# Turning the scans through DRAM: 256-byte writes into 16 KB rows, whole rows read back

## The chip, the cores and the metric

One core of a Trainium2 chip runs the whole program in one launch. The metric is the device time of that launch in microseconds. A run is repeated; one further execution is recorded by the hardware profiler. Engines are called as in the profile: PE (matmul), DVE (vector), ACT (scalar), POOL (GpSimd) and SP, which here only issues DMA transfers. SP and ACT each have one hardware DMA queue; both use the core's 16 DMA engines.

## The reference

An image `x` of shape (4, 48, 256, 256) in fp32 passes four residual layers, each `x = x + f(groupnorm(x))`. Layer 0 is a channel attention with depthwise convolutions, layer 1 a gated pointwise network, and layers 2 and 3, which the change concerns, are scans. A scan layer normalises its input and then runs four recurrences. Each step adds a 5-tap convolution of the line before (48 channels to 48) to the present line:

```python
def step(w, b):
    def f(carry, inp):
        nxt = inp + _conv1d(carry, w, b)
        return (nxt, nxt)
    return f
_, d_rest = jax.lax.scan(step(down_w, down_b), d0, xs[1:])     # rows, top to bottom
_, u_rest = jax.lax.scan(step(down_w, down_b), u0, seq)        # rows, bottom to top
_, r_rest = jax.lax.scan(step(right_w, right_b), r0, ws[1:])   # columns, left to right
_, l_rest = jax.lax.scan(step(left_w, left_b), l0, R[Ww - 2::-1])  # columns, right to left
```

The first two go over 256 rows, the last two over 256 columns of what the first two left. At the end the layer's own input is added (the residual).

## The kernel before

The program is one list of calls; a scheduler of the framework orders the instructions of each engine and adds the waits, except where `pin` keeps the written order. Layers 0 and 1 fill the first 2885 us and are interleaved. Then `scans` (from L1023) does reference layers 2 and 3 as `layer` 0 and 1 of one loop (L1143).

**One step.** A line (a row or a column) is held as 3 x 128 partitions: 8 positions along the line times 48 channels make 384, cut into three parts `m`; the free dimension is 128 long (32 positions within a piece times 4 images). `step` (L1084) is nine 128x128 fp32 matmuls into three PSUM banks and three DVE operations (L1103) that add bias and present line. The next step needs this step's result, so the steps form one chain over PE and DVE.

**Blocks.** 32 lines are a block, numbered J for rows and n for columns (`NBK` = 8). A block is 384 x 4096 values, 6.29 MB; 256 B, 64 values, is the part of one channel and row that lies in one piece of a column position. Buffers in SBUF: two big tiles of 3 x 4096 per partition (`c_big`), three slots of 4096 and three ring tiles of eight lines (`RING`). A ring tile of eight lines is filled (rows: normalised by ACT, L1172; L1170 shares the first one over ACT, DVE and POOL), stepped through in place, and spilled to DRAM in packets of 12 KB (rows `Dd`, L1241; columns `Rd`, L1353); the way back loads it again (L1298 on SP, L1452 on ACT). The last five stay (`KEEP`).

**From rows to columns and back**, all through DRAM, by plain DMAs with rearranged access patterns:

- Layer 2's input comes in row blocks from `x2r` (`load_x2`, L1122). Its residual is copied into column order by POOL (`copy_rows`, L1190: 12 copies of 1024 values a block into slots) and written to `Y0` in 24 DMAs a block (L1196), 256 B each, in steps of 2 KB.
- In the up scan ACT keeps each row in a big tile `u` (`keep_row`, L1253); a full block goes to `U` in packets of 2 KB (`write_U`, L1258; ten DMAs, `pieces_of_lines`). Column block n is read from `U` in packets of 256 B (`load_C`, L1266 for one block of rows, L1271 for several). POOL picks the columns out of it (`fetch`, L1314). For the last row block, the part that column block 0 needs is written and read first (L1301, L1302).
- In the left scan POOL adds the finished columns to the residual, the stage tile `s` (`add_line`, L1382). `stage_of` (L1360) loads it: in layer 2 from `Y0` in packets of 2 KB (L1372), in layer 3 from `Y1` in rows of 16 KB (L1369). In layer 2 the sum is the next layer's input: `write_Y` (L1384) writes it to `Y1` by column blocks in 16 KB rows, DVE takes its statistics (L1439), and `load_y` (L1128) reads row blocks of it in packets of 256 B, the first one in two parts (L1404 and L1457). `Y1` has rows of 4096 + 64 values, 48 of them for each of 64 groups, so that step from group to group is 48 x 4160 x 4 = 798,720 B. `U` and `Y0` have rows of exactly 16 KB and steps of 786,432 B from row to row of a block.
- In layer 3 the sum is the output (L1428).

**SP's queue.** Nearly all of these are issued by SP, in one order. A transfer that must wait for a buffer or for data holds up all that stand behind it. The instructions' waits show eight semaphores for these transfers in rotation, so that a transfer also waits for the one eight before it.

**The gated layer** (reference layer 1, `gated_layer` from L662) works on 32 items, each a band of 32 rows of one image. In a `tick`, SP loads `tok` (L751) and `xr` (L863), POOL sorts the result into `yr` (L897), and two DMAs write it to `x2r` (L909). Normally that write is put off to the beginning of the next tick; once the layer 0 work that it is interleaved with has ended (`alone`), the write is issued at once (L915).

Of the kernel before, what the change touches and what calls it, by code (L numbers as in the profile page):

```python
# [26 lines left out]
NPOS = 8  # L27
# [634 lines left out]
def gated_layer(ctx, tc, banks, p_small, x1, x2r, w1, w2, dw, ends, pw, cols, b2, k, coef1, coef2):  # L662
# [206 lines left out]
    def output(c, ip, alone):  # L869
# [45 lines left out]
        if alone:  # L915
            unwritten.pop()()
# [106 lines left out]
def scans(ctx, tc, x2r, out, wts, biases, dram, k, coef2, spare):  # L1023
# [104 lines left out]
    def load_y(t, J, n0=0, n1=NBK, queues=(nc.sync,)):  # L1128
        v = t.rearrange("p (m q e) -> p m q e", m=3, e=64)
        src = Y1.rearrange("q c e -> c q e")  # L1130
        for q, (j, c0, c1, m, p0, np_) in enumerate(pieces):
            at = 512 * j + 64 * J
            queues[q % len(queues)].dma_start(  # L1133
                v[p0 : p0 + np_, m, 8 * n0 : 8 * n1], src[c0:c1, 8 * n0 : 8 * n1, at : at + 64]
            )

    load_x2(xin, 0)
    Y0 = dram.tile([NPOS, 3 * 128, NBK, NBK, 64], F32, tag="Y0", name="Y0")
    Y1 = dram.tile([NBK * NPOS, C, SLOT + 64], F32, tag="Y1", name="Y1")
    both = (nc.sync, nc.scalar)  # L1140
    coefs = spread(coef2[:C].rearrange("p b s -> p (b s)"), "spread0")

    for layer in range(2):  # L1143
# [3 lines left out]
        U = dram.tile([NPOS, 3 * 128, NBK, NBK * 64], F32, tag=f"U{layer}", name="U")  # L1147
# [32 lines left out]
        def copy_rows(x, J):  # L1180

            def pieces_of(m):
                got = {}

                def one(b):
                    if b == 0:
                        got["t"] = slot_of.take("xr")
                    src = x.rearrange("p (m b i a g) -> p m b i g a", m=3, b=B, a=4, g=4)[:, m, b]
                    dst = got["t"][0].rearrange("p (i b g a) -> p b i g a", b=B, g=4, a=4)[:, b]
                    pin(nc.gpsimd.tensor_copy(dst, src))  # L1190

                def write():
                    t, h = got["t"]
                    v = t.rearrange("p (i n e) -> p i n e", i=NPOS, n=NBK)
                    for i in range(NPOS):
                        nc.sync.dma_start(Y0[i, chunk(m), :, J, :], v[:, slot_of_row(i)])  # L1196
                    give(h)

                return [lambda b=b: one(b) for b in range(B)] + [write]
# [10 lines left out]
        for a in range(32):  # L1210
            t, h = D[a]
            J, al = a // 4, a % 4
            if al == 0:
# [3 lines left out]
                if J + 1 < NBK:  # L1217
# [3 lines left out]
                    else:  # L1221
                        load_y(xnext[0], J + 1)
# [4 lines left out]
            if layer == 0 and al == 0:  # L1227
                copy_rows(xin, J)
            if a == 24:
                load_weights(ways.index((layer, 1)))  # L1230
            for i in range(NPOS):
# [6 lines left out]
                if copies and i % 2 == 0:  # L1238
                    copies.pop(0)()
# [11 lines left out]
        def keep_row(t, i, al, line):  # L1251
            v = t.rearrange("p (m i n a) -> p m i n a", m=3, i=NPOS, a=4)
            nc.scalar.copy(v[:, :, i, :, al], line)  # L1253

        def write_U(t, J, lo, hi):
# [385 lines left out]
```

## Time and profile before

| | us |
|---|---|
| median of 3 runs | 7228.17 |
| lowest, highest | 7224.77, 7231.26 |
| profiled execution, its own time | 7225.91 |
| its span in the profile | 7223.8 |
| PE busy in the span | 6764.5 |
| layers 0 and 1, about | 0 to 2885 |
| layer 2: down and up, right and left | 2900.0 to 3926.4, 3944.5 to 5018.9 |
| layer 3: down and up, right and left | 5063.5 to 6167.5, 6186.3 to 7215.4 |

In the profile a stretch of time is given as start:end in microseconds from the span's start. Busy times of an engine are summed over instructions; beside them stands their number. The DMA share is the mean busy share of the 16 DMA engines, and since packets on one engine overlap it can pass 1. A name such as `x<-Y` is what a transfer writes and reads, with buffer numbers left out: `Y` stands for `Y0` and `Y1`. "SPq" is the SP engine's DMA queue: the time in a row of it is how long SP was held issuing, not how long the data took. fp32 matmuls run in two passes, so nine of a step are 18 records.

### The profile page before, as it was taken

How to read it: one execution, taken by the hardware profiler on the slowest of the kernel's cores; microseconds unless marked ns; L12 is line 12 of the kernel's file. 1: busy time of each engine (PE TensorE's matmuls, PEld its weight loads, DVE VectorE, ACT ScalarE, POOL GpSimd, SP SyncE). 2: the span in 40 equal slices, each digit the busy share in tenths (PEclk: the TensorE clock that was granted, in tenths of full speed). 3: DMA queues.
4: the chain of work that ended last, by engine and by line, in shares of the span. 5: the costliest groups of instructions: out<-in, count | busy, mean ns of one | idle time of the engine just before them, and what ended most of it. 6: DMA issues, size and time to landing. Idle time of an engine off the chain costs nothing.

```text
span 7223.8 us, 125645 instructions
## 1 busy us (share of the span) xinstructions
PE 6764.5 (94%) x51694; PEld 5407.3 (75%) x51694; DVE 3764.6 (52%) x8893; ACT 1751.0 (24%) x1994; POOL 2143.7 (30%) x4268
## 2 busy tenths in 40 slices
PE   4999999999999965999999999996888999999999
PEld 3666653333333322999999999996888999899999
DVE  7887643355555555444444445664444444444444
ACT  0111112243434443444443000000535343100000
POOL 0101000033333344432000555764000000455677
PEclk9999999999999987999999999998999999999999
DMA  7651124566666675897567868898998267776675
GB/s 174 161 156 62 70 71 144 169 173 178 188 180 182 173 170 148 264 294 201 168 196 193 216 190 162 247 240 216 190 169 169 88 202 210 193 197 187 257 286 208
DMA packets 1177535, 1325.47 MB, mean 183 GB/s; under 512 B 831809, under 2 KB 1006401, under 8 KB 1125121
## 3 DMA queue, kind: packets, MB, share of 16 engines
q1 hardware_dynamic: 1163424, 1229.27, 63.0%
q10 hardware_dynamic: 13440, 87.84, 3.6%
q8 instruction: 406, 6.65, 0.4%
q14 instruction: 169, 1.38, 0.1%
q0 software_dynamic: 96, 0.33, 0.0%
HBM read 793.72 MB, written 522.19 MB: 182 GB/s over the span
## 4 chain that ended last, share of the span: by engine, by line
PE 55%; DMA 3%; SPq 3%; DVE 2%; POOL 1%; issue 1%; ACT 1%; ACTq 0%; POOLq 0%; DVEq 0%
PE ps L1097 54%; SPq L1133 2%; DMA D<-d 1%; ACT d L1172 1%; POOL s L1382 1%; DMA tok<-x 0%; DVE y L892 0%; DVE v L810 0%; POOL yr L897 0%; DMA near<-n 0%; DVE st L925 0%; PE ph L711 0%; DMA r<-R 0%; DMA x2r<-yr 0%; PE ptok L764 0%
## 5 line engine op out<-in xcount | busy, mean ns | idle before, releaser
L1097 PE MATMUL ps<-d,w 128*128 128x128 f32 (+1 forms) x18360 | 2070.3, 276 | 101.4 <-DVE d L1103 62.4
L1097 PEld LDWEIGHTS ps<-d,w 128*128 128x128 f32 x18360 | 2065.4, 193 | 106.2 <-DVE d L1103 66.1
L1097 PE MATMUL ps<-r,w 128*128 128x128 f32 (+1 forms) x18360 | 2071.7, 276 | 68.4 <-POOL r L1314 35.4
L1097 PEld LDWEIGHTS ps<-r,w 128*128 128x128 f32 x18360 | 2065.9, 193 | 74.3 <-DVE r L1103 37.9
L1103 DVE SCALAR_TENSOR_TENSOR d<-ps,b,d 128x128 f32<-128x128 f32 x3054 | 979.7, 349 | 1153.2 <-PE ps L1097 1074.8
L1382 POOL TENSOR_TENSOR s<-s,r 128x128 f32<-128x128 f32 x1536 | 745.4, 520 | 334.9 <-DVE r L1103 332.9
L1103 DVE SCALAR_TENSOR_TENSOR r<-ps,b,pre 128x128 f32<-128x128 f32 x1530 | 490.1, 348 | 581.3 <-PE ps L1097 581.1
L1103 DVE SCALAR_TENSOR_TENSOR r<-ps,b,r 128x128 f32<-128x128 f32 x1530 | 490.2, 348 | 459.6 <-PE ps L1097 432.5
L588 PE MATMUL py<-x1n,wy 128*96 128x512 f32 x1536 | 700.9, 606 | 2.4 <-POOL x2n L544 0.5
L1314 POOL COPY pre<-c 128x128 f32<-128x128 f32 x1530 | 558.4, 403 | 468.8 <-DVE r L1103 466.2
L1172 ACT ACTIVATE d<-x,spread 128x256 f32<-128x256 f32 x752 | 510.7, 826 | 543.3 <-DMA D<-d 325.7
L289 PE MATMUL acc<-moving,raw 128*48 128x240 f32 x4096 | 598.6, 367 | 11.6 <-DVE moving L275 9.9
L289 PE MATMUL acc<-moving,still 128*48 128x240 f32 x4096 | 588.8, 367 | 0.2
L1253 ACT COPY u<-d 128x384 f32<-128x384 f32 x510 | 448.8, 899 | 573.4 <-DVE d L1103 510.9
L588 PEld LDWEIGHTS py<-x1n,wy 128*96 128x96 f32 x1536 | 245.3, 165 | 418.6 <-issue 376.3
L1314 POOL COPY r<-c 128x128 f32<-128x128 f32 x6 | 2.4, 395 | 1689.2 <-DMA c<-U 1689.2
L611 DVE TENSOR_TENSOR y<-py,t 96x512 f32<-96x512 f32 x256 | 173.3, 677 | 565.5 <-PE py L597 565.5
L289 PEld LDWEIGHTS acc<-moving,raw 128*48 128x48 f32 x4096 | 317.6, 123 | 147.4 <-DVE moving L275 10.0
L289 PEld LDWEIGHTS acc<-moving,still 128*48 128x48 f32 x4096 | 320.3, 123 | 137.1 <-ACT acc_sb L306 1.5
L897 POOL COPY yr<-y 96x256 f32<-96x256 f32 x512 | 315.9, 661 | 202.0 <-DVE y L892 192.0
L597 PE MATMUL py<-x2n,wy 64*96 64x512 f32 x1536 | 361.9, 601 | 0.0
L597 PEld LDWEIGHTS py<-x2n,wy 64*96 64x96 f32 x1536 | 116.7, 158 | 234.4 <-issue 230.3
(194 smaller groups left out, 4244.9 us busy)
## 6 DMA issues: line engine op xcount, KB each, us to landing
t<-in_xc SPq DMA_DIRECT2D x64, 1536.0 KB
c<-U SPq DMA_DIRECT2D x348, 256.0 KB
D<-d SPq DMA_DIRECT2D x54, 1536.0 KB
d<-D SPq DMA_DIRECT2D x54, 1536.0 KB
R<-r SPq DMA_DIRECT2D x54, 1536.0 KB
r<-R ACTq DMA_DIRECT2D x54, 1536.0 KB
U<-u SPq DMA_DIRECT2D x84, 768.0 KB
sx<-in_x SPq DMA_DIRECT2D x128, 384.0 KB
```

What stands on the lines that cost most here:

```text
L289: nc.tensor.matmul(acc[i][64 * s : 64 * s + C], lhsT=still[i][:, w * C : (w + 1) * C], rhs=moving[:, i, w * C : (w + 5) * C], start=u == 0 ...
L588: nc.tensor.matmul(ps, lhsT=held["w"][0][:, dx], rhs=x1n[:, 2 * c : 2 * c + 2, dx : dx + W], start=dx == 0, stop=False)
L597: nc.tensor.matmul(held["ps"][q + 2 * s], lhsT=held["w"][1][here, dx], rhs=x2n[here, 2 * q : 2 * q + 2, dx : dx + W], start=False, stop=dx ...
L611: nc.vector.tensor_add(part, held["ps"][c], t1[:P, 2 * c : 2 * c + 2, :])
L897: nc.gpsimd.tensor_copy(yrs[c][:, :, 2 * i2 + ip, :].rearrange("p j (n a g) -> p j n a g", a=4, g=4)[:, :, :, al], y[:, i2, al].rearrange( ...
L1097: nc.tensor.matmul(ps[m][:, here], lhsT=w[:, n, :], rhs=old[:, q, there], start=first, stop=last)
L1103: nc.vector.scalar_tensor_tensor(new[:, m], ps[m], bias[:, m : m + 1], inp[:, m], ALU.add, ALU.add)
L1133: queues[q % len(queues)].dma_start(v[p0 : p0 + np_, m, 8 * n0 : 8 * n1], src[c0:c1, 8 * n0 : 8 * n1, at : at + 64])
L1172: pin(nc.scalar.activation(dst, src, AF.Identity, bias=g[:, 1:2], scale=g[:, 0:1]))
L1253: nc.scalar.copy(v[:, :, i, :, al], line)
L1314: nc.gpsimd.tensor_copy(dst[:, m].rearrange("p (J a b) -> p J a b", J=NBK, b=B), v[:, m, j, :, gl].rearrange("p J b a -> p J a b"),)
L1382: nc.gpsimd.tensor_add(v, v, line[:, m].rearrange("p (J a b) -> p J a b", J=NBK, b=B))
```

## The change

- `U`, `Y0` and `Y1` get one layout, that of `Y1`: 64 groups of 48 rows of 4096 + 64 values. There is a `U` and a `Y0` for each layer.
- All writes to them go through `scatter`: ten DMAs a block, each of up to 48 partitions times 64 packets of 256 B, in steps of 798,720 B from packet to packet. This takes in the writes to `U` and `Y1`, 2 KB and 16 KB packets before.
- All reads go through `gather`: three DMAs of 128 rows of 16 KB. Where less than a block is read (for the last row blocks of `U` and the first block of `Y1`), parts of these rows are.
- Layer 3's residual no longer comes from `Y1`: its input blocks, once in SBUF, are scattered to a second `Y0` as soon as a block begins.
- `copy_rows` makes 48 copies of 256 values a block, two a step, in the new order; its three writes are three, four and three scatter pieces.
- `keep_row` writes its row into another order of the same tile.
- At the turn to columns, only the first of the ten pieces is written ahead of the first column's read; the rest of the first column block is written and read next, on both queues.
- In the gated layer, only the last item's write is issued at once.

```diff
-        if alone:
+        if c + 1 == len(items):
             unwritten.pop()()
...
-    def load_y(t, J, n0=0, n1=NBK, queues=(nc.sync,)):
-        v = t.rearrange("p (m q e) -> p m q e", m=3, e=64)
-        src = Y1.rearrange("q c e -> c q e")
-        for q, (j, c0, c1, m, p0, np_) in enumerate(pieces):
-            at = 512 * j + 64 * J
-            queues[q % len(queues)].dma_start(
-                v[p0 : p0 + np_, m, 8 * n0 : 8 * n1], src[c0:c1, 8 * n0 : 8 * n1, at : at + 64]
+    ROW = SLOT + 64
+    scratch = lambda name: dram.tile([NBK * NPOS, C, ROW], F32, tag=name, name=name)
+    both = (nc.sync, nc.scalar)
+    thirds = lambda t: [t[:, m * SLOT : (m + 1) * SLOT] for m in range(3)]
+
+    def scatter(dst, at, ts, lo=0, hi=64, queues=(nc.sync,), some=pieces):
+
+        for n, (pos, c0, c1, m, p0, np_) in enumerate(some):
+            queues[n % len(queues)].dma_start(
+                dst.rearrange("q c e -> c q e")[c0:c1, lo:hi, at(pos) : at(pos) + 64],
+                ts[m].rearrange("p (q e) -> p q e", e=64)[p0 : p0 + np_, lo:hi],
             )
 
+    def gather(ts, src, block, lo=0, hi=SLOT, inner=None, queues=(nc.sync,)):
+
+        rows = src.rearrange("(n i) c e -> n (i c) e", i=NPOS)[block]
+        for m in range(3):
+            to, of = ts[m][:, lo:hi], rows[chunk(m), lo:hi]
+            if inner:
+                to, of = (x.rearrange("p (j e) -> p j e", e=512)[:, :, inner[0] : inner[1]] for x in (to, of))
+            queues[m % len(queues)].dma_start(to, of)
...
-                    v = t.rearrange("p (i n e) -> p i n e", i=NPOS, n=NBK)
-                    for i in range(NPOS):
-                        nc.sync.dma_start(Y0[i, chunk(m), :, J, :], v[:, slot_of_row(i)])
+                    scatter(Y0, lambda j: 512 * J + 64 * j, {m: t}, some=[p for p in pieces if p[3] == m])
                     give(h)
 
-                return [lambda b=b: one(b) for b in range(B)] + [write]
+                return [lambda b=b, al=al: one(b, al) for b in range(B) for al in range(4)] + [write]
...
-                        load_y(xnext[0], J + 1)
+                        gather(thirds(xnext[0]), Y1, J + 1)
...
-            if layer == 0 and al == 0:
-                copy_rows(xin, J)
+            if al == 0:
+                if layer == 0:
+                    copy_rows(xin, J)
+                else:
+                    scatter(Y0, lambda j: 512 * j + 64 * J, thirds(xin))
...
+            v = t.rearrange("p (m n i e a) -> p m n i e a", m=3, n=NBK, i=NPOS, a=4)
+            nc.scalar.copy(v[:, :, :, i, :, al], line.rearrange("p m (n e) -> p m n e", n=NBK))
+
+        def write_U(t, J, **how):
+            scatter(U, lambda j: 512 * j + 64 * J, thirds(t), **how)
...
                 if row == 40:
                     near = big_tile("c")
-                    load_C(near[0], 0, 2, NBK)
+                    gather(thirds(near[0]), U, 0, inner=(128, 512))
                 if row == 32:
-                    load_C(near[0], 0, 1, 2)
+                    gather(thirds(near[0]), U, 0, inner=(64, 128))
...
-        write_U(ut, 0, 0, 64)
-        load_C(near[0], 0, 0, 1)
-        write_U(ut, 0, 64, 512)
+        write_U(ut, 0, hi=8, some=pieces[:1])
+        gather(thirds(near[0]), U, 0, hi=512, inner=(0, 64), queues=both)
+        write_U(ut, 0, hi=8, some=pieces[1:], queues=both)
+        gather(thirds(near[0]), U, 0, lo=512, inner=(0, 64), queues=both)
+        write_U(ut, 0, lo=8)
...
-                load_C(near[0], n + 1, 0, NBK)
+                gather(thirds(near[0]), U, n + 1)
...
-            if layer == 1:
-                for m in range(3):
-                    nc.sync.dma_start(s[m], Y1.rearrange("(n i) c e -> n (i c) e", n=NBK)[n, chunk(m), :SLOT])
-                return s, hs
-            for i, c0, c1, m, p0, np_ in pieces:
-                nc.sync.dma_start(
-                    s[m].rearrange("p (j e) -> p j e", j=NPOS)[p0 : p0 + np_],
-                    Y0[i].rearrange("(j c) n J e -> c j n (J e)", c=C)[c0:c1, :, n, :],
-                )
+            gather(s, Y0, n)
             return s, hs
...
+        def write_Y(s, n, **how):
+            scatter(Y1, lambda i: 512 * n + 64 * i, s, **how)
...
-                load_y(xnext[0], 0, 1, NBK)
+                gather(thirds(xnext[0]), Y1, 0, lo=512)
...
-            write_Y(s, 0, 0, 64, both)
-            load_y(xnext[0], 0, 0, 1, both)
-            write_Y(s, 0, 64, 512)
+            write_Y(s, 0, hi=8, queues=both)
+            gather(thirds(xnext[0]), Y1, 0, hi=512, queues=both)
+            write_Y(s, 0, lo=8)
```

## The prediction

> **What bounds the kernel now.** I read the page first, then PE's busy time stage by stage, then who ended PE's waits in the bad stages, then the SP queue there, and last the DMA engines in windows that hold one kind of transfer. The page says that PE is the bound and that the DMA traffic is mostly tiny:
>
> ```profile
> PE 6764.5 (94%) x51694; PEld 5407.3 (75%) x51694; DVE 3764.6 (52%) x8893; ACT 1751.0 (24%) x1994; POOL 2143.7 (30%) x4268
> DMA packets 1177535, 1325.47 MB, mean 183 GB/s; under 512 B 831809, under 2 KB 1006401, under 8 KB 1125121
> ```
>
> The busy table by stretches (start:end, length, PE busy (matmuls), ..., clock, DMA share, GB/s):
>
> ```profile
> 2900.00:3926.40 1026.40, 1026.32 (x9172) 1025.83 (x9172) 490.24 (x1530) 448.52 (x616) 188.86 (x96) 1.00 0.72 217
> 3926.40:3944.50 18.10, 0.80 (x2) 0.50 (x2) 0.30 (x1) 0.87 (x1) 1.77 (x6) 0.61 0.93 210
> 3944.50:4820.00 875.50, 875.49 (x7801) 873.54 (x7802) 489.74 (x1422) 0.00 (x0) 529.70 (x1281) 1.00 0.82 213
> 4820.00:5018.90 198.90, 164.73 (x1380) 163.59 (x1378) 108.96 (x291) 0.00 (x0) 120.01 (x249) 0.91 0.77 217
> 5018.90:5063.50 44.60, 4.43 (x24) 3.96 (x24) 15.13 (x34) 3.25 (x6) 2.73 (x3) 0.54 1.16 190
> 5063.50:5580.00 516.50, 454.00 (x3922) 450.34 (x3923) 209.81 (x653) 242.01 (x333) 1.69 (x3) 0.92 1.06 181
> 6167.50:6186.30 18.80, 0.80 (x3) 0.51 (x3) 0.35 (x1) 0.86 (x1) 1.81 (x6) 0.55 0.95 213
> ```
>
> First row: 510 scan steps in 1026.4 us, PE never idle, so 2.01 us a step and 64.4 us for a block of 32 rows. All that a change of transfers can win in the scans is PE's idle time: 17 us at each of the two turns from rows to columns, 34 in the end of layer 2's left scan, 40 between the layers, 62.5 in layer 3's down scan, 171 in all. Who ends it in layer 3's down scan, and the SP queue in one block of it (start, length, line, transfers):
>
> ```profile
> PE ps L1097 <- DVE d L1103: 62.4, 14, 17.2
> ...
> 5297.49 0.32 SPq L1241 DMA_DIRECT2D D<-d  x1
> 5297.87 30.67 SPq L1133 DMA_DIRECT2D x<-Y  x9
> 5328.65 17.43 SPq L1241 DMA_DIRECT2D D<-d  x3
> ```
>
> DVE is blamed, but the chain of work runs SP L1133, D<-d, ACT L1172: spills of finished rows stand in SP's queue behind 256-byte reads of Y1, a ring tile is not freed, and ACT fills the next rows late. The rates, mean or in 40 bins, in the order: Y0's 256 B writes in 2 KB steps (2908); U's 2 KB writes (3483); Y0's 2 KB reads (4405, idle after half); the 256 B reads of Y1 (5092); U's 256 B writes at the turn (6171.5); whole rows of 16 KB (6700):
>
> ```profile
> GB/s 0 0 0 0 0 145 290 288 296 284 288 285 287 293 287 293 282 285 293 287 293 287 282 291 291 288 291 284 284 295 285 295 287 278 295 288 291 288 282 289
> ...
> DMA packets 2135, 4.16 MB, mean 260 GB/s; under 512 B 113, under 2 KB 113, under 8 KB 2134
> ...
> GB/s 188 111 159 151 138 144 156 144 151 161 121 139 210 206 223 236 228 157 152 149 52 10 0 7 0 0 0 13 0 0 0 0 0 7 0 0 0 0 13 0
> ...
> DMA packets 13531, 3.47 MB, mean 116 GB/s; under 512 B 13529, under 2 KB 13529, under 8 KB 13529
> ...
> DMA packets 4306, 1.07 MB, mean 237 GB/s; under 512 B 4306, under 2 KB 4306, under 8 KB 4306
> ...
> GB/s 393 131 164 262 459 426 393 426 459 426 459 393 393 459 426 492 426 393 393 492 426 426 459 393 426 426 459 426 393 426 360 98 33 0 0 16 0 0 0 0
> ```
>
> Size alone does not set the rate: 256 B goes at 288 in short steps and at 116 when read in steps of 798,720 B.
>
> [...]
>
> **The change part by part.** One pass over the tensor is 50.3 MB, a block 6.29 MB (24,576 packets of 256 B). The unknown is W, the time of one block's scatter: 256 B writes in steps of 798,720 B. No run shows it. Fast end: Y0's writes, 6.29/288 = 22 us. Slow end: the slowest reads in the same steps, 6.29/116 = 54. Between: U's 2 KB writes and Y0's 2 KB reads have the same pattern on the DRAM side (16 KB pitch, steps of 786,432 B) and ran at 260 and about 150, so writes bear long steps 1.7 times better. A whole Y1 block is read in some 38 us (its blocks alternate) to 54, mean 46, 137 GB/s; times 1.73 is 237, which is also what the 256 B writes at the turn did. I take W = 26.5 and keep 22 and 54. A gather of a block in whole rows is 6.29/425 = 15 us; four spills or refills of 128 packets of 12 KB are 4 x 3.8 = 15.
>
> Layer 2 down: loads 15 + spills 15 + W = 57 of 64.4 a block: no stall. POOL's copies become 48 of 256 elements a block instead of 12 of 1024; at the 661 ns of L897's copy of that size 32 us instead of 24, hidden, POOL works 189 us in this stage.
>
> Both up scans: U's writes take W instead of 24. ACT's copy (L1253, 899 ns) of row 31 waits for the write of block 1 and must then catch up 32 rows in 28.8 us, so the write may take 35.6 us: nothing at 26.5 + 2; 7 us a layer at W = 40. No wait on PE follows otherwise, refills run five tiles ahead.
>
> The two turns to columns: the first gather waits for one small write instead of ten, and the second line for the rest (3,072 packets, 3.5 us, twice 2 us landing, 2,688 packets read). The first step can start early, the second cannot. I give 3 us each: -6 (bounds -14 and +2, since a 2,688-packet write stands ahead of the second gather on SP).
>
> Right scans: whole rows of U instead of 256 B; PE was never idle: 0.
>
> Layer 2 left: the stage's gather falls from 42 us (2 KB at 150) to 15, Y1's write rises from 15 to W. Per block 15 + 15 + 26.5 = 56.5 instead of 72; the buffer's write and refill in a row are 41.5 instead of 57. The 34 us of idle came from stages landing late (POOL, then r<-R): -26, 8 left.
>
> Between the layers: 42 us of 256 B reads go. Seven eighths of block 0 need 13 us in 14 KB rows, behind POOL's last addition in the SP order; the rest follows with 3.3 us of writes, 3 of reads and two landings, then ACT, DVE and POOL normalise, 4 us. 27 instead of 44.6: -17. The statistics alone need to 5036, so not over -24.
>
> Layer 3 down: a spill now stands behind two gathers less (they are ahead of the previous spill) and the ten scatters: 5 + 26.5 instead of 38 to 54 us; blocks with 38 to 45 stalled 3, those with 54 some 15. So nearly nothing a block. At its start a backlog: rest of Y1 (23), Y0 (26.5), gather (15) from 5035, so the first spill lands near 5104; ring reuse wants it by about 5085: 20 us. 22 instead of 62.5: -40.
>
> Gated layer: the block writes go to the next tick. In SP's queue a tok load stood behind such a write until 2566.1, 2632.5, 2695.2, 2760.3; the load ahead of it left 8, 5, 4 and 4 us earlier, and the built order has tok before the write. -8 of at most -21; at worst 0, as the last write stays put.
>
> Layer 3 right and left: 0 (PE full). Sum -6 - 26 - 17 - 40 - 8 = -97. The profiled execution took 7225.9 (span 7223.8 and 2.1 around), 2.3 under the median of 7228.2: 7129 by its time, 7131 by the median. I forecast **7133**.
>
> **Rivals.** *Writes as slow as the reads*, slower: at W = 46, layer 2 down needs 76 of 64.4 (+93), layer 3 down 8 x 12 + 30 = 126 instead of 62.5 (+64), left 7 x 12 + 8 = 92 instead of 34 (+58), ACT's catching up 2 x 12 (+24), less 31 for turns, between the layers and gated layer: +208, 7436. It decides from W = 38 (165 GB/s): there 68 of 64.4 gives +29, -4, -1 and +9 against the -31 of turns, between the layers and gated layer. For it: same addresses, 116 to 165 GB/s as reads, and one pass of 256 B more. Against: 260 to 150. *The stalls only change their cause*: W is right, but spills still stand behind whole scatters and stages behind Y1's writes; only turns, between the layers and gated layer win, and 8 of the rest: -6 - 17 - 8 - 8 = -39, 7189. For it: SP issues in order and the scatter of a block is one burst. *It does not do what it says*: the built order has all scatters and gathers as written; I give it nothing.
>
> **How the numbers follow.** The forecast has 0.50, changed causes 0.17 (0.14 faster, 0.03 same), W between 37 and 39 0.07 (half same, half slower), slow writes 0.26. A measurement tells about 0.2%, 14 us: faster 0.64, same 0.06, slower 0.30. Its own range is 7085 (all stalls but the statistics gone) to 7170. The 8 in 10: 7085 to 7310, W = 41 (71 a block: +53, +20, +20, +16, -31, 7306); above lies about 0.15, below 0.04.
>
> **What would show it.** Packets under 512 B near 1.03 million; Y0, U and Y1 scatters at 230 GB/s or more; no wait of PE in layer 2 down; under 30 us of idle in layer 3 down, most of it in its first block; under 12 in layer 2 left; 27 between the layers. Wrong if a scatter runs under 165 GB/s, or if PE's waits move to D<-d in layer 2 or to u<-d before the turns.

## The result, and the profile after the change

The changed kernel takes 7304.2 us (median of 4 runs, 7302.1 to 7312.8) against 7227.0 us: a ratio of 1.0108, 95% interval 1.0091 to 1.0126. It is slower by 77 us where 97 us less were forecast. The page of the changed kernel's profile has the same two lines that were shown of before:

```profile
PE 6785.3 (93%) x51694; PEld 5446.9 (75%) x51694; DVE 3765.8 (52%) x8893; ACT 1744.2 (24%) x1994; POOL 2146.1 (29%) x4556
DMA packets 1309084, 1375.76 MB, mean 188 GB/s; under 512 B 1024800, under 2 KB 1196320, under 8 KB 1247840
```

The packets under 512 bytes are the 1.03 million foretold, so the change does what it says. The time is lost where PE waits; a stretch in which it stands still is called a stand below. The table of busy times by stretches of the changed kernel, cut at the ends of the scans (start:end, length, PE busy, ..., clock, DMA share, GB/s):

```profile
2876.90:3903.70 1026.80, 1026.05 (x9172) 1025.96 (x9172) 490.27 (x1529) 441.98 (x611) 191.83 (x385) 1.00 0.77 223
3903.80:3925.10 21.30, 4.25 (x20) 3.96 (x19) 0.80 (x3) 5.51 (x9) 2.95 (x9) 0.69 0.91 191
...
4436.00:5018.90 582.90, 534.12 (x4611) 532.03 (x4610) 353.87 (x949) 0.00 (x0) 369.29 (x766) 0.95 0.68 207
5018.90:5094.70 75.80, 4.44 (x25) 3.96 (x24) 15.81 (x36) 3.27 (x6) 3.30 (x6) 0.52 0.84 227
5094.70:5735.40 640.70, 540.62 (x4591) 535.38 (x4592) 246.29 (x764) 270.93 (x372) 0.85 (x2) 0.90 0.80 224
5735.40:6248.10 512.70, 512.68 (x4592) 512.48 (x4590) 244.99 (x765) 221.52 (x256) 0.00 (x0) 1.00 0.67 176
```

In order: layer 2 down and up, never idle; its turn to columns; its left scan; the stand between the layers; layer 3 down; layer 3 up, never idle again. The third, fourth and fifth rows hold the loss. Idle time is not all of it: layer 3's down scan (fifth row) is 128 us longer than the up scan in the row below it; of these PE is idle for 100, and for the same number of steps it is busy 28 us longer (540.6 against 512.7), at a mean granted clock of 0.90 instead of 1.00.

The following table gives such lengths for every kernel of this study, from the first to the last matmul of a scan (the first scan's first steps are counted in "down"). A scan without a stall is 513 us, "down" of layer 2 some 524 with its beginning. "Turn and right" is the stand at the turn plus the right scan. All up scans and layer 3's left scan are 512.7 to 513 everywhere. The columns are read from one profiled execution of each kernel. The start of the scans lies between 2861 and 2876 in all kernels that have the gated layer's edit, so differences under 15 us in that column are not read as an edit's doing.

| kernel | median us | scans start | L2 down | L2 turn and right | L2 left | between layers | L3 down | L3 turn and right |
|---|---|---|---|---|---|---|---|---|
| before | 7227 | 2888.6 | 525.0 | 535.2 | 556.5 | 45.8 | 591.4 | 536.1 |
| changed | 7304 | 2867.3 | 524.0 | 534.6 | 580.7 | 75.8 | 640.8 | 532.2 |
| e1 | 7356 | 2870.7 | 569.2 | 533.3 | 571.5 | 87.0 | 643.1 | 534.1 |
| e2 | 7209 | 2887.7 | 524.9 | 535.5 | 559.6 | 53.2 | 570.7 | 536.2 |
| e3 | 7207 | 2872.3 | 525.5 | 533.8 | 556.5 | 45.6 | 591.8 | 533.7 |
| e4 | 7364 | 2864.4 | 524.1 | 540.2 | 578.4 | 86.9 | 680.8 | 538.5 |
| e5 | 7262 | 2870.6 | 526.5 | 532.5 | 571.9 | 74.9 | 609.3 | 532.0 |
| e6 | 7168 | 2879.8 | 524.3 | 536.9 | 554.7 | 46.0 | 538.8 | 536.6 |
| e7 | 7187 | 2868.6 | 524.2 | 532.1 | 571.6 | 73.9 | 535.7 | 533.7 |
| e8 | 7266 | 2868.4 | 524.0 | 532.1 | 577.0 | 74.4 | 608.2 | 534.5 |
| e9 | 7168 | 2872.9 | 525.5 | 532.5 | 573.8 | 49.6 | 537.1 | 532.0 |
| e10 | 7082 | 2863.5 | 525.3 | 532.6 | 512.7 | 22.2 | 537.9 | 536.0 |
| e11 | 7145 | 2866.2 | 524.0 | 533.2 | 556.0 | 45.2 | 537.4 | 533.6 |
| e12 | 7232 | 2862.3 | 524.6 | 534.6 | 577.8 | 75.5 | 573.8 | 533.2 |
| e13 | 7145 | 2868.2 | 525.4 | 535.1 | 512.7 | 22.2 | 601.9 | 535.5 |
| e14 | 7168 | 2861.4 | 524.3 | 534.0 | 572.1 | 50.2 | 536.7 | 531.8 |
| e15 | 7090 | 2876.1 | 524.1 | 535.6 | 512.7 | 22.2 | 536.2 | 535.9 |
| e17 | 7123 | 2871.4 | 524.5 | 533.7 | 512.7 | 65.0 | 535.7 | 532.3 |
| e18 | 7259 | 2874.7 | 524.6 | 533.6 | 571.9 | 74.3 | 607.2 | 532.2 |

The first two rows are the account: 21 us won ahead of the scans, 1 in layer 2 down and 4.5 at the turns; 24 lost in layer 2's left scan, 30 between the layers, 49 in layer 3's down scan. 24 + 30 + 49 - 21 - 1 - 4.5 = 77.

What layer 3's down scan waits for shows in SP's queue of the changed kernel (start, length, line, transfers; the lines of before are in the prediction):

```profile
5203.27 0.32 SPq L1255 DMA_DIRECT2D D<-d  x1
5203.63 0.43 SPq L1148 DMA_DIRECT2D x<-Y  x1
5204.11 44.57 SPq L1136 DMA_DIRECT2D Y<-x  x10
5248.79 8.30 SPq L1255 DMA_DIRECT2D D<-d  x3
...
5286.53 36.66 SPq L1136 DMA_DIRECT2D Y<-x  x10
5323.31 10.98 SPq L1255 DMA_DIRECT2D D<-d  x3
```

The spill of a finished ring tile stands behind ten scatters, 45 us in one block and 37 in the next. Both halves of this, the burst and its two speeds, are taken apart below. The two speeds appear in the DMA engines while nothing but a scatter runs, for the blocks of 5204 and 5287 (26 us of each):

```profile
DMA packets 14156, 3.62 MB, mean 139 GB/s; under 512 B 14154, under 2 KB 14154, under 8 KB 14154
...
DMA packets 19971, 5.12 MB, mean 197 GB/s; under 512 B 19968, under 2 KB 19968, under 8 KB 19968
```

### The profile page after: what moved, and what is told of

It reads as the page before. It is cut to its first block, busy times and chain, and to the rows that moved or that the text cites. A ratio compares the mean times of both kernels' runs of the same rounds, so it can differ in the third digit from the quotient of the medians.

```text
span 7300.6 us, 125352 instructions
## 1 busy us (share of the span) xinstructions
PE 6785.3 (93%) x51694; PEld 5446.9 (75%) x51694; DVE 3765.8 (52%) x8893; ACT 1744.2 (24%) x1994; POOL 2146.1 (29%) x4556
## 4 chain that ended last, share of the span: by engine, by line
PE 52%; SPq 4%; DMA 3%; POOL 2%; ACT 1%; issue 0%; DVE 0%; ACTq 0%; POOLq 0%; DVEq 0%
PE ps L1097 52%; SPq L1136 3%; POOL s L1375 1%; DMA D<-d 1%; ACT d L1183 1%; DMA Y<-s 0%; DMA r<-R 0%; POOL yr L897 0%; DMA U<-u 0%; ACT u L1267 0%; DMA s<-Y 0%; DMA near<-n 0%; DMA c<-U 0%; DMA x2r<-yr 0%; SPq L1148 0%
```

## The experiments

Runs marked "tiles at 512" carry the filling of e5. The time of a block's scatter is taken from the trace, from the start of its first 256-byte packet to the end of the last of its 24,576, for blocks of `U` and layer 3's `Y0` whose ten transfers leave without a long wait between them. Each ratio is taken against the kernel before on the same chip; the times of runs from different chips are compared only roughly.

### The place of a tile in SBUF: e1, e2, e4, e5, e6, e18

In the changed kernel blocks alternate with the buffer they leave from. The two big tiles start at bytes 20,960 and 176,640 of a partition, the slots at multiples of 512. Every block from the first tile is slow, U, Y1 and Y0 alike; before's reads of Y1 into the same two tiles alternate too, 54 and 37 us. e1 moves the first tile:

```diff
+    fill = pool("c_fill0", 1)
+    fill.tile([128, 8], F32, tag="fill", name="fill")
     big = [pool("c_big0", 1)]
     wp = pool("c_w", 2)
     work = pool("c_work", 1)
+    fill = pool("c_fill1", 1)
+    fill.tile([128, 8], F32, tag="fill", name="fill")
```

> The changed kernel with 32 bytes of filling ahead of the first big tile in SBUF and 32 more ahead of the ring tiles: the first big tile starts at 20,992 bytes of a partition instead of 20,960 (a multiple of 64 instead of 32 above one), the second stays at a multiple of 64. Theory S (a 256-byte packet that starts 32 bytes off a multiple of 64 in SBUF is slow; it is the blocks in the first big tile that took 43 us): all scatters of U, Y1 and of layer 3's Y0 take 33 us, their packets 17 ns on average instead of 24.5; idle of PE in layer 3's down scan falls from about 100 us to 40, the end of layer 2's left scan from 47 to 25, between the layers from 77 to 68; 7225 us, between 7195 and 7250. Rival D (it is the place in DRAM that makes odd blocks slow, their address being 256 bytes off): the odd blocks stay at 43 us and the time at 7304 within 10. Rival B (the burst in SP's order counts, not its speed): the scatters quicken, but the time falls by less than 25, to 7280 or more.

Measured: 7356.1 us, ratio 1.0182 (1.0168 to 1.0196). The first tile's blocks became quick, 33 us, but the second tile's, moved by 64 bytes, took 40 to 43, and layer 2's down scan, whose slots moved as well, grew by 45 us. So the start counts, as theory S has it, but its number, 64, was wrong, and the time rose where a fall of 79 us was expected. e2 is the same edit on the kernel before:

> The kernel before with the same 64 bytes of filling. Theory S: its 256-byte reads of Y1 into the first big tile (about 53 us a block, 45 ns a packet) become as quick as those into the second (37 us, 28 ns); idle of PE in layer 3's down scan falls from 62 us to 25, some 10 more are won in the left scan of layer 2 and between the layers: 7180 us, between 7160 and 7200. Rival D: nothing changes, 7227 within 10.

7209.4 us, ratio 0.998 (0.9973 to 0.9988): 14 us under its own before, less than a third of what was expected: reads of a block into the first tile fell from 54 us to 40, those into the second rose from 37 to 48. e4 has 8 elements of filling ahead of the second big tile only:

> The changed kernel with 32 bytes of filling ahead of the second big tile only, so that both big tiles start 32 bytes off a multiple of 64. Theory S: every scatter out of a big tile takes 43 us at 24.5 ns a packet; in layer 3's down scan a block has gather 15, spills 15, scatter 43 = 73 us of transfers for 64.4 us of work in every block instead of every other, some 8 x 9 more: 7375 us, between 7340 and 7430. Rival D: the time stays at 7304 within 10, and blocks go on alternating.

7363.5 us, ratio 1.0192 (1.0178 to 1.0206); every block from either tile 42 to 45 us; layer 3's down scan 680.8. Rival D falls: the layout in DRAM is the same in all of these. e5 and e6 fill 32 bytes ahead of the first tile and 480 (`[128, 120]`) ahead of the ring tiles, after and before the change:

> The first runs showed that the start of a tile in SBUF sets the rate of a scatter: 33 us a block where the tile starts at a multiple of 512 bytes, 41 to 43 where it starts 64, 32 or 480 bytes above one; filling the first big tile up moved the second one and the slots off their places. Here 32 bytes of filling stand ahead of the first big tile and 480 ahead of the ring tiles, so that both big tiles and the three slots start at multiples of 512; the rest is the changed kernel. Theory S (start in SBUF): every scatter 33 us, no alternation; the four slow blocks of layer 3's down scan lose 10 us each and PE's idle there falls from 100 us to 55, the left scan and the gap between the layers lose 15 together: 7245 us, between 7220 and 7265. If the place in SBUF only goes along with something else (the buffer's turn in the order, other traffic), slow blocks stay and the time is 7290 or more.

> The kernel before with both big tiles and the slots at multiples of 512 bytes. Theory S: its 256-byte reads of Y1 take 37 us for every block (54 and 37 by turns before), its 256-byte reads of U in the right scans gain as well, but are hidden; PE's idle in layer 3's down scan falls from 62 us to 25: 7190 us, between 7180 and 7205, and 10 to 25 under the run with only the first big tile moved (7209). Otherwise 7209 or more.

e5: 7261.6 us, ratio 1.0045 (1.0032 to 1.0057), all those blocks 32 to 34 us, layer 3's down scan 31.5 us shorter than in the changed kernel. e6: 7168.4 us, ratio 0.9916 (0.9902 to 0.9929): 61 us won with 512 bytes of filling, 53 of them in layer 3's down scan, more than expected. Thus alignment alone makes the changed kernel 43 us better and the kernel before 61: it explains much of the time, but not why the change loses. e18 leaves the slots and the second tile 256 bytes above a multiple of 512 (`[128, 56]`):

> The changed kernel with the first big tile at a multiple of 512 bytes of SBUF (20,992), and the slots and the second big tile 256 bytes above one. Starts 0, 32, 64 and 480 bytes above a multiple of 512 gave 17.2, 19.2, 19.4 and 24.5 ns a packet. Theory 256 [...]: the blocks from the second tile take 33 us at 17.2 ns as from the first, and the time is 7262 within 12. Theory 512 (multiples of 512 count): these blocks take 40 us or more, and the time is 7320 or more, as with 64 bytes.

7258.9 us, ratio 1.0039 (1.0019 to 1.0058), those blocks 32 to 35 us, all blocks at 16.8 to 17.4 ns a packet. So 256 bytes above a multiple of 512 is as good as the multiple itself, as theory 256 expected of these blocks. Of the starts tried, 0, 32, 64 and 224 bytes above a multiple of 256, only the first is quick; 128 was not tried.

### The burst in SP's queue: e7, e12

```diff
-                    scatter(Y0, lambda j: 512 * j + 64 * J, thirds(xin))
+                    copies.extend(
+                        lambda p=p, t=thirds(xin), J=J: scatter(Y0, lambda j: 512 * j + 64 * J, t, some=[p]) for p in pieces
+                    )
...
-                for _ in range(2):
+                for _ in range(2 if layer == 0 else i % 2):
```

> The kernel with all tiles at multiples of 512 bytes, and layer 3's scatter of Y0 issued one piece at every second row step, 20 row steps for ten pieces, in place of ten pieces at the head of the block. Theory Q (a spill of a finished ring tile waits in SP's queue behind the whole scatter, which is the stall): PE's idle in layer 3's down scan falls to 30 us or less, nearly all in its first block: 25 to 50 us under the kernel with tiles at 512 alone. Rival T (the engines' time is what is short: gather 15, spills 15 and scatter 33 are 63 us of a block's 64.4): the stall only moves, the time is within 8 us of that kernel.

Measured: 7186.9 us, ratio 0.9942 (0.993 to 0.9955), 75 us under e5; layer 3's down scan fell from 609.3 to 535.7. SP's queue in e7:

```profile
5198.08 16.20 SPq L1140 DMA_DIRECT2D Y<-x  x4
5214.39 3.60 SPq L1261 DMA_DIRECT2D D<-d  x1
5218.03 6.91 SPq L1140 DMA_DIRECT2D Y<-x  x2
5225.05 5.20 SPq L1261 DMA_DIRECT2D D<-d  x2
```

Spills now go between the pieces. The same bytes at the same rate no longer stall: theory Q stands, T falls: PE's idle in that scan is 15 us in e7 against 69 in e5. e12 is this edit on the changed kernel, its tiles where they were:

> The changed kernel, tiles where they were, with layer 3's scatter of Y0 in pieces at every second row step. With tiles at 512 the pieces took idle of PE in layer 3's down scan from 68 us to 14. Theory Q (order alone): the same here, from 100 to 20: 7225 us, between 7215 and 7235. Rival B (both count: with scatters of 33 and 43 us by turns the transfers of a block are 63 and 73 us for 64.4 us of work, 29 us too many over the scan): idle 45 or more: 7250 us or more.

7232.1 us, ratio 1.0006 (1.0 to 1.0013): layer 3's down scan 573.8 us, 67 better than the changed kernel and 38 worse than e7. The time lies in theory Q's range, but PE's idle in that scan is 40 us: not the 20 of order alone, and under the 45 or more of rival B. Beside e7's 15 it shows that both count, the order more.

### The stand between the layers: e8, e9

The eight semaphores that the transfers use in turn, here called completion counters, are shared by SP and ACT (in the changed kernel's trace numbers 100, 101, 110 to 112 and 114 to 116): a transfer of SP can have to wait until one of ACT, eight before it, has landed. From 4480 to 4930 SP's writes of Y1 waited 203.7 us in all, 16 times, for r<-R, which ACT issues. SP's queue at the end of the changed kernel's left scan, which ends at 5018.9:

```profile
4957.89 110.47 SPq L1136 DMA_DIRECT2D Y<-s  x21
5069.09 1.29 SPq L1148 DMA_DIRECT2D x<-Y  x3
5070.42 2.28 SPq L1136 DMA_DIRECT2D Y<-s  x4
5085.59 3.33 SPq L1148 DMA_DIRECT2D x<-Y  x2
```

The 21 are the rest of block 2 (nine), all of block 1 and the first two of block 0; the next layer's load of seven eighths can't leave before them. Two causes were tried. e8, with tiles at 512, has POOL issue layer 2's refills:

```diff
-                nc.scalar.dma_start(flat(R[new][0]), Rd[new])
+                (nc.gpsimd if layer == 0 else nc.scalar).dma_start(flat(R[new][0]), Rd[new])
```

> The kernel with all tiles at multiples of 512 bytes, and the refills of ring tiles in layer 2's left scan issued by POOL in place of ACT. SP's and ACT's transfers take eight completion counters by turns, so a piece of Y1's scatter waits until the transfer eight before it has landed, and where that is a refill, for the ring tile which that refill waits for. Theory C (this coupling paces Y1's scatter at PE's speed, so that block 1 is not written when the scan ends): the scatter of a block takes 33 to 45 us from its first piece, SP waits for r<-R no longer (230 us in the changed kernel), PE's stand between the layers falls from about 70 us to 45 and the left scan's idle by 10 or more: 30 to 50 us under the kernel with tiles at 512 alone. Rival: the refills stand behind POOL's additions and come late, PE waits for r, the time is the same or longer.

7265.9 us, ratio 1.0049 (1.0035 to 1.0063): the stand is as long, 74.4, and the left scan 5 us longer than in e5. Theory C fails as a cure; the time is the same, as the rival had it. SP's longest wait was now 119.5 us for a scatter of Y1 itself, which pointed to the pieces of block 0 on ACT's queue. The changed kernel's trace agrees: SP issues nothing from 5006.4 to 5020.9, with 14 pieces of blocks 2 and 1 to go, and the next leaves after ACT's piece of 5019.0, which took the same counter, 101. e9 is e7 with

```diff
-            write_Y(s, 0, hi=8, queues=both)
-            gather(thirds(xnext[0]), Y1, 0, hi=512, queues=both)
+            write_Y(s, 0, hi=8)
+            gather(thirds(xnext[0]), Y1, 0, hi=512)
```

> The kernel with tiles at 512 and Y0 in pieces (7187 us), and the last block of Y1 in layer 2 written and read by SP alone, where five of its ten first pieces went through ACT. In the order of the program these five stand among the pieces of block 2, and a transfer waits for the one eight before it; so most pieces of blocks 2 and 1 on SP waited for pieces that can only leave after the scan's last row. Theory L (this is why the stand between the layers is 74 us, not 45): blocks 2 and 1 are written by the scan's end, the stand falls to 35 to 45 us: 7152 us, between 7142 and 7165. Rival M (block 1 is late since POOL's additions are late): the stand stays at 65 or more, 7180 or more.

7167.9 us, ratio 0.9919 (0.9906 to 0.9933): the stand fell from 73.9 to 49.6, some two thirds of what theory L gave it; the time is 3 us above the theory's range. ACT's five pieces did hold SP up; the rest is block 1's scatter, late anyway.

### One part at a time: e3, e10, e11, e13, e15, e17, e14

e3 has only the gated layer's line of the change, e11 that line and tiles at 512:

> The kernel before with only the gated layer's part of the change (a block's write leaves one tick later). In the changed kernel the scans started 22 us earlier than in the kernel before. If that is this edit's doing alone, 7227 - 22 = 7205 us, between 7198 and 7212. If it came from the other parts (fewer or other transfers in the gated layer's tail), 7227 within 6. My own forecast gave this part 8 us: 7219.

> The kernel before with tiles at 512 and the gated layer's part of the change. The two alone gave -61 and -23 against the kernel before; if they do not touch each other 7168 - 16 to 23 = 7149, between 7143 and 7158. If the start of the scans was already earlier by the tiles' places (it was 9 us earlier in the profile of that kernel), only 8: 7160.

e3: 7207.0 us, ratio 0.9976 (0.9967 to 0.9986), the scans start 16 us earlier. e11: 7145.0 us, ratio 0.989 (0.9875 to 0.9905), 82 us under its own before, where the two alone gave 61 and 16: they add up. e10 is e5 with Y1 as before; layer 2's Y0 is still scattered and gathered, with its pieces in the order of Y1's rows, which POOL's additions follow (522 ns each on average in the left scan, 526 in e5):

```diff
-            scatter(Y1, lambda i: 512 * n + 64 * i, s, **how)
+            dst = Y1.rearrange("(n i) c e -> n (i c) e", n=NBK)[n, :, :SLOT].rearrange("f (j e) -> f j e", j=NPOS)
+            for m in range(3):
+                queues[m % len(queues)].dma_start(
+                    dst[chunk(m), :, lo:hi], s[m].rearrange("p (j e) -> p j e", j=NPOS)[:, :, lo:hi]
+                )
...
-                    scatter(Y0, lambda j: 512 * j + 64 * J, thirds(xin))
...
-            gather(s, Y0, n)
+            gather(s, Y1 if layer else Y0, n)
```

> The changed kernel with tiles at 512, but Y1 as in the kernel before: written in rows of 16 KB, read in 256-byte packets, and the residual of layer 3 taken from Y1's rows, so that the pass of Y0 in layer 3 is gone. What stays of the change is U in both layers, Y0 of layer 2 and the gated layer's part. Theory P (the forecast's own step for layer 2's left scan: a gather of 15 us in place of 42 takes the stalls away, were it not for Y1's scatter): idle of PE in that scan falls from 33 us in the kernel before to 10, with 46 between the layers and 13 in layer 3's down scan as in the kernel before with tiles at 512: 7168 - 23 - 10 = 7135 us, between 7125 and 7148. Rival R (there the stalls never came from the gather's length but from refills, completion counters and POOL's catching up): idle stays at 28 or more: 7153 to 7170.

Measured: **7082.2 us**, ratio 0.9804 (0.979 to 0.9817), better than both kernels. The table by stretches for its left scan, the stand and layer 3 down:

```profile
4428.50:4941.00 512.50, 512.50 (x4592) 512.50 (x4591) 352.61 (x945) 0.00 (x0) 371.55 (x762) 1.00 0.71 264
4941.00:4963.20 22.20, 8.50 (x68) 7.90 (x66) 16.07 (x37) 0.25 (x1) 4.96 (x11) 0.67 0.43 131
4963.20:5501.00 537.80, 519.15 (x4549) 516.68 (x4550) 244.61 (x763) 275.82 (x377) 3.82 (x4) 0.98 0.84 174
```

PE is never idle in the left scan, and the stand is half of before's, though the 256-byte reads are back. SP's queue in e10 shows why:

```profile
4907.30 27.79 SPq L1159 DMA_DIRECT2D x<-Y  x10
4946.60 4.30 SPq L1391 DMA_DIRECT2D Y<-s  x3
4952.30 13.65 SPq L1159 DMA_DIRECT2D x<-Y  x5
```

With Y1 written on time, the load of seven eighths of the next layer's first block starts 34 us ahead of the scan's end, and only the last eighth is left for the stand. Theory P was right in cause and gave 53 us too little: idle fell to 0, not 10, and it had left the stand at 46. e13 is the same edit on the changed kernel, tiles where they were; e15 is e11 with only layer 2's Y0 in the new form, U as before:

> The changed kernel with Y1 as before and without layer 3's pass of Y0, tiles where they were: U, layer 2's Y0 and the gated layer's part of the change, nothing else. With tiles at 512 it ran 7082 us with no idle in layer 2's left scan, 22 us between the layers and 12 in layer 3's down scan. Theory: the left scan needs no place at 512, since its gathers and writes are whole rows of 16 KB; layer 3's down scan reads Y1 in 256-byte packets again at 54 and 37 us by turns and stands 62 us as in the kernel before: 7082 + 50 = 7132 us, between 7120 and 7145. If the gain in the left scan hung on the places as well, its idle is 15 or more, and the time over 7145.

> The kernel before with tiles at 512, the gated layer's part, and layer 2's Y0 in the new form (scattered in the down scan, whole rows read in the left scan); U and Y1 as before. It lacks only U's new form against the kernel of 7082 us. My forecast gave U's form 3 us at each turn and nothing elsewhere: 7088 us. The profiles show 17.0 us of stand and a right scan of 516.2 us with the old U, 10.4 and 522.2 with the new one, the same sum: 7082 within 6. If U's 256-byte writes helped or hurt in another place, it lies outside 7074 to 7094.

e13: 7145.3 us, ratio 0.9882 (0.9869 to 0.9896): the left scan's gain does not hang on the places in SBUF; layer 3 down is 64 us longer than in e10. e15: 7090.1 us, ratio 0.9808 (0.9795 to 0.9821). The interval overlaps with e10's, and in the profiles the 8 us more lie in the start of the scans (2876 against 2864), so no worth of U's new form, which e15 lacks, is shown; at the turns it is at most 3 us (535.6 and 535.9 us against 532.6 and 536.0). Against e11, Y0 of layer 2 alone in the new form takes 43 us off the left scan and 23 off the stand. e17 is e10 with Y1's rows cut into as many transfers as the scatter has:

```diff
-                            write_Y(s, n)
+                            rows = Y1.rearrange("(n i) c e -> n (i c) e", n=NBK)[n, :, :SLOT]
+                            for pos, c0, c1, m, p0, np_ in pieces:
+                                nc.sync.dma_start(rows[48 * pos + c0 : 48 * pos + c1], s[m][p0 : p0 + np_])
```

> The kernel of 7082 us (Y1 as before, tiles at 512), with the write of a block of Y1 cut into ten transfers of whole rows, the same cuts as the scatter's, in place of three: the same bytes, rows and packets. Theory C (what stands in the left scan is the number of transfers: ten and three a block with four refills go over eight completion counters, so a write waits for a refill, the refill for a ring tile, and the next residual's gather stands behind it; SP waited 254 us for r<-R with ten pieces and not at all with three): SP waits for r<-R again by 100 us or more, and PE's idle in the left scan rises from 0 to 25 or more: 7110 us or more. Theory W (it is the scatter's small packets, 33 us or more of the engines' time in place of 15): SP's waits stay small and PE's idle at 0 to 5: 7082 within 8.

7123.5 us, ratio 0.9863 (0.9846 to 0.9879). SP's waits from 4480 to 4930, which e10 has none of for r<-R (in all, times, longest):

```profile
SPq L1450 <- DMA r<-R: 198.0, 15, 17.9
SPq L1450 <- POOL s L1386: 96.2, 10, 41.4
SPq L1152 <- DMA r<-R: 63.3, 4, 18.1
```

They are as long as in the changed kernel (204 and 57 us), yet the left scan stays at 512.7; only the stand grows, from 22 to 65. So the number of transfers lengthens the stand between the layers, by the waits for counters as far as these show, and it does not by itself stall the left scan: both theories were half right.

The chain of work in the changed kernel's left scan shows the way of a stall (start, length, what):

```profile
4872.29 14.73 DMA s<-Y
...
4897.81 16.06 POOL s L1375 x34
4913.89 10.16 DMA r<-R
```

The residual of block 1 lands late, POOL must catch up, the ring tile it adds from comes free late, and the refill that needs this tile ends PE's wait. SP's issue of the last residual's gather in the changed kernel, e9, e17 and e10:

```profile
4954.38 3.46 SPq L1148 DMA_DIRECT2D s<-Y  x3
...
4950.26 1.29 SPq L1152 DMA_DIRECT2D s<-Y  x3
...
4869.46 20.19 SPq L1152 DMA_DIRECT2D s<-Y  x3
...
4778.66 1.28 SPq L1152 DMA_DIRECT2D s<-Y  x3
```

The first column that needs it is ready at 4943.1, 4940.9, 4892.4 and 4884.2. So the gather leaves 105 us ahead with three transfers of rows a block (e10), 23 us ahead with ten (e17), and 11 and 9 us late with ten scatters (changed, e9). In the last four blocks of the changed kernel POOL starts 17, 9, 27 and 21 us behind the column; in e17 and e10 it never does. The number takes most of the lead, and the scatter's small packets the rest. In e8 POOL never starts more than about 1 us behind, yet the scan stalls for 47 us; there POOL's additions stand in one queue with the refills, so e8 does not test this.

e14 meant to space Y1's scatter over the next block:

```diff
-                            write_Y(s, n)
+                            later.extend(lambda p=p, s=s, n=n: write_Y(s, n, some=[p]) for p in pieces)
```

> The kernel of 7168 us (tiles at 512, Y0 in pieces, last block of Y1 on SP alone) with the scatters of Y1 spaced too: one piece at every second row step of the next block. Theory Q (in the left scan also the burst counts: ten pieces at once wait for completion counters that refills hold, 60 to 90 us of SP's queue for a block's 64, and the gather of the next residual behind them comes late): idle of PE in the left scan falls from 42 us to 15 or less, the stand between the layers stays at 50 within 8: 7138 us, between 7125 and 7150. Rival: the gather or the refills are late in any order, since the scatter itself keeps SP and the engines: idle 30 or more, 7155 to 7180.

7168.5 us, ratio 0.9914 (0.99 to 0.9927), the same as e9. Its built order of SP's queue is that of e9, piece by piece, so it tested nothing.

## Why the prediction was wrong, point by point

- **W, "26.5 us" a block.** A block takes 32 to 34 us from a tile at a multiple of 256 bytes and 42 to 45 from the first big tile, 38 on average: the point at which the forecast said it decides. The term was mis-sized by its factor: "writes bear long steps 1.7 times better" came from U's writes and Y0's reads. In the tiles concerned a block takes 37 and 54 us to read (before) and 33 and 43 to write, a factor of 1.1 and 1.3. Averaging the reads to 46 ("its blocks alternate") hid the clue to the second speed, but did not make W small. A scatter at 139 GB/s is also under the 165 that the forecast named as a sign of being wrong. At W = 38 the rival's formula gives about 0, not +77, so W alone was not it. That the top of the stated range, W = 41 and 7306 us, lies 2 us from the result is luck: it puts 53 us in layer 2's down scan, which lost nothing.
- **Layer 3 down, "nearly nothing a block ... 22 instead of 62.5: -40".** It failed: +49. What it names, spills behind ten scatters, is what happened; the size was wrong. From the spill before the burst to the one behind it the step has 5 + 26.5 us; the lines above have 45.5 and 37.6, the trace of before has 42.5 (5216.2 to 5258.7) and 31.2 (5297.5 to 5328.7). And it is steep: with 31 to 32 us in each block (e6) PE is idle for 15 us in this scan, with 37.5 (e5) for 69. Even with every scatter at 33 us (e5) the scan is 609 us; with spills between the pieces it is 536 (e7). The burst's order is 74 of it, its rate 31.5; in the changed kernel's tiles spacing it alone gives 67 (e12).
- **Between the layers, "27 instead of 44.6: -17".** It failed: +30. The step counted the gather from POOL's last addition and forgot that it must also wait for the scatters of blocks 2 and 1, which no longer were three quick row writes. Ten transfers in place of three cost 43 us (e17); ACT's pieces are 24 of the changed form's stand (e9).
- **Layer 2 left, "-26".** It failed: +24. Its half on the gather is right and too small: without Y1's scatter the scan loses all its stalls, 43 us (e10, e13, e15). The step "the buffer's write and refill in a row are 41.5 instead of 57" failed: in e9 SP issues a block's ten scatters over 60 to 91 us, not 26.5, since they wait for counters that refills hold (198.7 us of SP's waits from 4480 to 4930 end on r<-R), and the next gather stands behind them. Number of transfers alone doesn't stall PE (e17); whether small packets in three transfers would, was not tried.
- **"All that a change of transfers can win in the scans is PE's idle time ... 34 in the end of layer 2's left scan".** Too little: e10 wins 44 us there, since PE's busy time falls as well, from 523 to 513, while the granted clock of that scan rises from 0.97 to 1.00. The forecast priced every stall at its idle time alone.
- **Gated layer, "-8 (max -21)".** -16 alone (e3), -21 in the changed kernel, the same within the spread of the starts. Right in sign, mis-sized: the end nearer to the bound was true.
- **Turns, "3 each".** -0.6 and -3.9: right. The landing, taken as 2 us, shows in the chain of before: a small write of U, issued by 3934.9, released SP 2.27 us later. PE's first stand fell from 17 to 11, and a second of 5 to 6 us came two columns later, where the forecast saw that the second column's load can't start early.
- **Layer 2 down and both up scans, no stall.** Right for the changed kernel. ACT's catching up after a late write of U, priced at 7 us a layer for W = 40, cost nothing visible at 43 to 45; in e4, where also the last blocks of U are slow, the two turns lengthen by 5 to 6 us.
- **The rival "writes as slow as the reads"** named the side, not the places: it put most of its loss in layer 2's down scan, which lost nothing.

In one sentence: layer 2's Y0, written in small pieces and read in whole rows, wins more than was said (e15 against e11), but Y1's and layer 3's scatters put small transfers where in-order queues had quick ones, and the three stretches that they touch are together 103 us longer than before. What stays open is whether Y1's small packets would stall the left scan in three transfers instead of ten.

## What to carry to other kernels

When a pass over data is moved from reading small pieces to writing them, ask what waits for the write, and what stands behind it in its queue: here reads ahead of time had a block of slack (the gather of e10 left 105 us before its data were needed) and writes at the end of a scan had none (the stand behind the last of Y1 grew by 30 us). The same step can help one tensor and hurt the next: layer 2's Y0 gained (66 us in the left scan and the stand, e15 against e11), since its writes lie in the down scan, where PE never stood for them (524.1 us against 524.0). Count transfers as well as bytes where completion counters go round (ten in place of three made the stand 65.0 us instead of 22.2, e17 against e10), and spread a burst between the short transfers that others wait for (74 us, e7 against e5). If equal blocks alternate in time, 33 and 43 us here, look where their buffers start before averaging. A stall cost more here than the time PE stood still, since the steps after it were slower too: 128 us for 100 of idle time in layer 3's down scan.

## What the runs showed of the hardware

A 256-byte packet out of SBUF took, on average in whole blocks, 17.2 ns from a start at a multiple of 256 bytes (the changed kernel's second tile, e5, e18), 19.2 at 32 above (e4), 19.4 at 64 above (e1) and 24.5 at 224 above (the tile at 20,960 in the changed kernel); a block of 24,576 packets took 33, 42.5, 41 and 43 us. For packets into SBUF it was 28 to 32 ns at a multiple of 512 (before's second tile), 41 to 42 at 64 above (e2) and about 45 at 224 above (before's first tile). The times of whole blocks do not follow those of packets: the start at 32 above takes longer for a block than that at 64 above, 42.5 against 41 us, and nearly as long as that at 224. Why a start counts in this way was not shown.

After a stand PE's steps were slower for a while: in layer 3's down scan of the changed kernel a step that starts at 5499.3, just after a stand, takes 3.6 us at a granted clock of 0.54, one at 5504.9 takes 2.0 at 1.00. The scans without a stall, before and after the change, show 1.00 throughout. Before's layer 2 left scan, with 33 us of idle time, has 0.97 on average, the changed kernel's layer 3 down scan, with 100 us, 0.90.
